# Places of a mixture of experts, due earlier and closer together in the order of an attention kernel

## The chip, the cores and the metric

The kernel runs on one core of one Trainium2 chip. The metric is the device time of one execution in microseconds (us). Before the change the median of 9 runs is 812.9 us (811.49 to 815.56).

## The reference

The input x has 2 batches of 2048 tokens of width 256, all in float32. First comes attention with 4 heads of width 64, with two layer norms ahead of it and a root-mean-square norm on queries and keys; its output is layer-normed and added to x. Then comes a mixture of 8 experts: each token goes through the one expert that its scores choose, and the result is layer-normed and added.

```python
x = x + _layernorm(_L0_attn_ref(_layernorm(x), ...))

scores = jnp.einsum('bsh,eh->bse', x, gate_w)
chosen = jnp.argmax(scores, axis=-1)
onehot = jax.nn.one_hot(chosen, gate_w.shape[0], dtype=x.dtype)
expert_out = jnp.einsum('bsh,efh->bsef', x, expert_w)
ffn = x + jnp.einsum('bsef,bse->bsf', expert_out, onehot)

x = x + _layernorm(ffn)        # ffn is fed with _layernorm(x)
```

## The kernel before, in words

Tokens stand in 32 tiles of 128. The attention is 256 steps (batch, block of 512 queries, pair of heads, tile of keys), taken two at a time: 128 loop passes, called slots here. In each slot the program emits, in this order: the scores of the next slot (`s`, L1049, on TensorE, or PE) with their exponentials (`p`, L1057, on ScalarE, or ACT); the addition of this slot's `p` into the running sum (`acc`, L1092 and L1094, on VectorE, or DVE); whatever side work is due (`between(now)`); and the product of `p` with the values (`po`, L1103, on PE). Instructions are emitted in a manual order, and each engine takes its own in that order and waits where an operand isn't there yet. So side work that is emitted ahead of a slot's `po` delays the `po` if it has to wait.

The side work is a set of Python generators. A queue holds each with the slot at which it begins. A `yield` ends its share of a slot; `yield later(...)` does too, while `then(...)` goes on in the same slot. In `places` the first part (the gather) is emitted as soon as the generator is taken up.

What the side work is:

- `project`: norm, queries, keys and values of a tile.
- `tokens`: a tile's output product (`py`, L802), norm, residual `x2`, expert scores, pick, and norm `x2n`. A tile of a group writes `x2` and `x2n` to memory.
- `order(gr)`: for a group of tiles, sorts the tokens by expert. Group A is tiles 0 to 15, group B tiles 16 to 27. It begins when the last tile of the group has its pick. Its first part (rank matmuls at L588 and L589, then some 24 small DVE operations) is one slot's work; its second part (L640 to L671, DVE, ending with the comparisons `inrow`) is the next slot's. Two `yield`s follow. Then PE turns it into the list of source rows (`src`, L681: 32 matmuls in group A, 24 in group B) and DVE casts it (L688). It then queues the places and the collects.
- `places(gr, j)`: one tile of 128 places that have one expert; A has 23, B has 19. GpSimd (POOL) gathers the rows (`rows`, L707), the SyncE queue (SP) loads the expert's weights (`ring`, L721), PE turns the rows (`pt_g`, L729), ACT copies them (`xT`, L734), PE multiplies (`pe`, L739; `peA`, `peB` by group), ACT copies out (L749), the norm follows (DVE L387 to L389; the root on POOL, L383 and L400, while attention runs, and on ACT, L404, or wholly on ACT, L414 to L424, after it), ACT scales (L755), and SP writes the result `fn` (L756).
- `collect(gr, t)`: gathers a tile's results from `fn` (L777, POOL), adds the residual (L789, DVE) and writes the output (L793). In group B it waits until all of `fn` is written.

The last four tiles, 28 to 31, are in no group: each goes through all 8 experts (L871, two products of four experts each) and DVE picks (L886, L888). After the last slot, `finish()` emits what is left in an order that it plans with a cost and a wait that each step states (`Next("POOL", 1.3)` and so on), and with counts of free buffers (`have`). So that order is a result of planned times, not of measured ones.

A place is due at slot `at`, which goes up by 1 for each place (by 0.34 past the attention's end).

Of the kernel before, what the change touches and what calls it, by code (L numbers as in the profile page):

```python
# [25 lines left out]
def kernel(  # L26
# [18 lines left out]
    B, N, D = x.shape  # L45
# [4 lines left out]
    NT = N // P  # L50
# [3 lines left out]
    QT4 = KB // P  # L54
# [227 lines left out]
    def bounded_path():  # L282
# [70 lines left out]
        def ps_m(name):  # L353
            return psum.tile([P, KB], F32, tag="ps_m", name=name, bufs=3)
# [20 lines left out]
        def later(*args, **kw):  # L375
            return Next(*args, later=True, **kw)
# [16 lines left out]
        def norm(src, name, shift=None, give=""):  # L393

            mv, rs = moments(src, name)
            if shift is None:
                shift = small.tile([P, 1], F32, tag="shift", name=f"shift_{name}")
            if attending:
                rsqrt(rs, mv[:, 1:2], 1.0, LN_EPS, ALU.add)
                nc.gpsimd.tensor_scalar(shift, mv[:, 0:1], rs, -1.0, ALU.mult, ALU.mult)  # L400
            else:
                yield then("ACT", 0.2, give=give)
                sd = small.tile([P, 1], F32, tag="sd", name=f"sd_{name}")
                nc.scalar.activation(sd, mv[:, 1:2], AF.Sqrt, bias=eps)  # L404
                yield then("DVE", 0.4)
                nc.vector.reciprocal(rs, sd)
                nc.vector.tensor_scalar(shift, mv[:, 0:1], rs, -1.0, ALU.mult, ALU.mult)
            return rs, shift

        def norm_on_act(dst, src, name):  # L410

            a = small.tile([P, 4], F32, tag="onact", name=f"onact_{name}")
            total, less, square, sd = (a[:, i : i + 1] for i in range(4))
            nc.scalar.activation(dst, src, AF.Copy, accum_out=total)  # L414
            nc.scalar.activation(less, total, AF.Copy, scale=-1.0 / D)
            sq = wk.tile([P, 2 * D], F32, tag="sq", name=f"sq_{name}", bufs=1)
            nc.scalar.activation(sq[:, :D], dst, AF.Square, bias=less, accum_out=square)
            nc.scalar.activation(sd, square, AF.Sqrt, bias=eps, scale=1.0 / D)
            yield then("DVE", 0.2, give="m")
            rs = small.tile([P, 1], F32, tag="rs", name=f"rs_{name}")  # L420
            nc.vector.reciprocal(rs, sd)
            yield then("ACT", 0.2)
            shift = small.tile([P, 1], F32, tag="shift", name=f"shift_{name}")
            nc.scalar.activation(shift, less, AF.Copy, scale=rs)  # L424
            return rs, shift
# [126 lines left out]
        def load_experts():  # L552
            nonlocal weD
            v = kv.tile([P, NT, DG], F32, tag="V", name="ring").rearrange("p t d -> p (t d)")
            ring.extend(
                v[:, i * KB : (i + 1) * KB].rearrange("p (c d) -> p c d", d=D)
                for i in range(NT // NCH)
            )
            xg = wk.tile([P, 6, D], F32, tag="rows", name="rows", bufs=1)
            rows.extend(xg[:, i, :] for i in range(6))  # L560
            weD = kv.tile([P, NCH, E, D], F32, tag="KT", name="weD")
            for e in range(E):
                nc.sync.dma_start(out=weD[:, :, e, :], in_=weTd[e])
            yield
# [17 lines left out]
        def order(gr):  # L582


            T, S, n = gr.T, gr.S, gr.name
# [89 lines left out]
                    ALU.is_equal,  # L675
                )
            yield
            yield
            ps = ps_m(f"src{n}")
            for t in range(T):  # L680
                nc.tensor.matmul(  # L681
# [5 lines left out]
                )  # L687
            nc.vector.tensor_copy(gr.src, ps[:, :S])  # L688

            at = now + 1  # L690
            for j in range(S):
                at += 0.34 if at >= len(steps) // PAIR + lead else 1
                g = opens(early(places(gr, j)), Next("POOL", 1.3), 0, lambda: 0.0 if ring and rows else None)
                queue.append((at, g))
            for t in range(T):
# [6 lines left out]
        def places(gr, j):  # L702

            n = f"{gr.name}{j}"
            assert ring and rows, "a tile of places with no room"
            w, xg = ring.pop(0), rows.pop(0)
            nc.gpsimd.indirect_dma_start(  # L707
                out=xg,
                out_offset=None,
                in_=gr.x2n[:, :],  # L710
                in_offset=bass.IndirectOffsetOnAxis(ap=gr.src[:, j : j + 1], axis=0),
                bounds_check=gr.T * P - 1,
                oob_is_err=False,
            )
            e = nc.values_load(
                gr.exp[0:1, j : j + 1],
                engines=[mybir.EngineType.SP],
                min_val=0,
                max_val=E - 1,
            )  # L720
            nc.sync.dma_start(  # L721
                out=w, in_=weTd[bass.ds(e, 1)].rearrange("e p c d -> p (e c) d")
            )
            yield later("PE", 0.3, 3.0, take="mx")
            if attending:
                yield later("PE", 0.3, take="mx", give="mx")
            pt = ps_m(f"pt_g{n}")
            for c in range(NCH):
                nc.tensor.transpose(  # L729
                    pt[:, c * P : (c + 1) * P], xg[:, c * P : (c + 1) * P], ident  # L730
                )
            yield then("ACT", 0.4)
            xT = wk.tile([P, NCH, P], F32, tag="xT", name=f"xT{n}", bufs=4)
            nc.scalar.copy(xT, pt[:, :D].rearrange("p (c n) -> p c n", n=P))  # L734
            rows.append(xg)
            yield later("PE", 0.9, take="mf", give="m")
            pe = ps_m(f"pe{n}")[:, :D]
            for c in range(NCH):
                nc.tensor.matmul(  # L739
                    pe, xT[:, c, :], w[:, c, :], start=(c == 0), stop=(c == NCH - 1)  # L740
                )
            ring.append(w)
            f = spare.pop() if spare else None
            own = f is None
            if own:
                f = wk.tile([P, D], F32, tag="fl", name=f"f{n}", bufs=5)
            yield then("ACT", 1.5 if j % 3 == 0 else 0.4, give="x")
            if attending or j % 3:
                nc.scalar.copy(f, pe)  # L749
                yield then("DVE", 0.7, give="m")  # L750
                scale, shift = yield from norm(f, f"f{n}")
            else:
                scale, shift = yield from norm_on_act(f, pe, f"f{n}")
            yield later("ACT", 0.6)
            nc.scalar.activation(f, f, AF.Identity, bias=shift, scale=scale)  # L755
            nc.sync.dma_start(out=gr.fn[j * P : (j + 1) * P, :], in_=f)  # L756
            gr.left -= 1
            gr.written = max(gr.written, clock + 2.5)
            yield later("", 0.0, 2.5)
            if not own:  # L760
                spare.append(f)
            yield later("", 0.0, give="f")
# [33 lines left out]
        def tokens(bt, qb, j, oTs, gr):  # L796
# [40 lines left out]
            if gr:  # L837
                gr.met += 1
                if gr.met == gr.T:
                    queue.append((now, order(gr)))  # L840
                    queue.sort(key=lambda q: q[0])
# [61 lines left out]
        def early(g):  # L903

            firsts.add(g)
            return g
# [84 lines left out]
        def opens(g, step, order, gate=None):  # L991


            opening[g], order_of[g] = step, order
            if gate:
                gates[g] = gate
            return g

        batches = [Batch(b) for b in range(B)]
        for t in range(NT):  # L1000
            queue.append((t, project(batches[0], t)))
        steps = [
            (b, qb, c, kc)
            for b in range(B)
            for qb in range(NKB)
            for c in range(NCH)
            for kc in range(NT)
        ]

        groups = []  # L1010
        for name, first, n in (("A", 0, NT), ("B", NT, NT - QT4)):
            groups.append(Group(name, n))
            groups[-1].first = first
        queue.append((NT + NT * NKB + 4, load_experts()))
        queue.append((0, weights()))
        queue.append((3, scale_g()))
# [2 lines left out]
        PAIR = 2  # L1019
# [94 lines left out]
        attending = True  # L1114
        now = lead = 0
# [4 lines left out]
        for g in range(len(steps) // PAIR):  # L1120
# [5 lines left out]
            lead = now - g  # L1126
# [9 lines left out]
            if kc == NT - 1:  # L1136
# [5 lines left out]
                if c == NCH - 1:  # L1142
                    tt = b * NT + qb * QT4
                    gr = next((g for g in groups if g.first <= tt < g.first + g.T), None)
# [9 lines left out]
        attending = False  # L1154
# [333 lines left out]
    with tc.If(chosen != 0) as cmp:  # L1488
        with ExitStack() as path:
            bounded_path()  # L1490
# [44 lines left out]
```

## Time and profile before

| what | value |
|---|---|
| median of 9 runs | 812.9 us |
| profiled execution, its time | 812.81 us |
| profiled execution, its span | 811.0 us |
| PE busy | 761.1 us, 94% |
| DVE busy | 640.0 us, 79% |
| ACT busy | 448.8 us, 55% |
| POOL busy | 326.7 us, 40% |
| last `po` of the attention ends | 722.65 us |

The profile is of one execution. Times in its timeline are from the span's start; a row gives the start, the duration, the engine, the line, the operation, output and input tiles with their shapes, and how many equal ones follow each other. A bracket at the end of a row is the idle time of the engine before it and what ended it. PEclk is the clock that TensorE was granted, as a share of full speed. The ends of matmuls are modelled.

### The profile page before, as it was taken

Reading aid. Unit: us, or ns where it says so; the run is one execution under the profiler, and the core shown is the slowest. Engines: PE = TensorE matmul, PEld = TensorE weight load, DVE = VectorE, ACT = ScalarE, POOL = GpSimd, SP = SyncE. Lnnn points to the kernel's source line nnn. Section 1 sums busy time; section 2 is a strip of 40 time slices with the busy share of each in tenths; the row PEclk is TensorE's granted clock in tenths of the full one; section 3 lists DMA queues with packets and bytes.
Section 4 is the critical chain, followed back from the end, with each engine's and each line's share of the span. In section 5 each row is a group of like instructions: output and inputs, shape, how many; then the busy total and the mean of one; then the engine's idle time right before and its main releaser. Section 6 shows DMA issues by size and latency. Waiting matters only on the chain.

```text
span 811.0 us, 10279 instructions
## 1 busy us (share of the span) xinstructions
PE 761.1 (94%) x3169; PEld 319.4 (39%) x3169; DVE 640.0 (79%) x1380; ACT 448.8 (55%) x699; POOL 326.7 (40%) x336
## 2 busy tenths in 40 slices
PE   6999999999999999999997999999999997985794
PEld 4555434433433433333332434444433232433451
DVE  3767678698879878788899958788789899953767
ACT  3666555556665665655554466656665534453741
POOL 4634411144353334242242236757454453244014
PEclk9999999999999999999999999999999998996897
DMA  4100111200100000000411423432222332436136
GB/s 127 54 27 26 52 66 52 65 27 20 46 20 20 20 14 20 20 21 24 126 33 46 131 66 117 120 114 87 58 66 85 117 98 81 135 119 185 53 98 185
DMA packets 48150, 57.58 MB, mean 71 GB/s; under 512 B 5868, under 2 KB 39416, under 8 KB 48088
## 3 DMA queue, kind: packets, MB, share of 16 engines
q1 hardware_dynamic: 41528, 44.65, 17.4%
q0 software_dynamic: 3568, 9.32, 4.7%
q10 hardware_dynamic: 2992, 2.88, 1.2%
q8 instruction: 27, 0.44, 0.2%
q14 instruction: 35, 0.29, 0.1%
HBM read 37.69 MB, written 19.14 MB: 70 GB/s over the span
## 4 chain that ended last, share of the span: by engine, by line
PE 76%; DVE 12%; issue 4%; ACT 3%; DMA 3%; POOL 1%; SPq 0%; DVEq 0%; POOLq 0%; ACTq 0%
PE s L1049 25%; PE po L1103 24%; PE pqk L463 7%; PE pv L472 4%; DVE acc L1094 3%; PE py L802 3%; PE peA L739 3%; PE pt_qk L500 2%; PE sm L1065 2%; PE peB L739 2%; PE pt_x L450 1%; DVE acc L1073 1%; PE pe L871 1%; DMA fgA<-fnA,posA 1%; DMA gk_all<-in_L_attn_k_gamma_dram 1%
## 5 line engine op out<-in xcount | busy, mean ns | idle before, releaser
L1057 ACT ACTIVATE p<-s,nbound 128x1024 f32<-128x1024 f32 x256 | 271.0, 1110 | 182.8 <-PE s L1049 182.8
L1094 DVE TENSOR_TENSOR acc<-acc,p 128x1024 f32<-128x1024 f32 x224 | 273.7, 1222 | 11.5 <-ACT p L1057 1.2
L1049 PE MATMUL s<-QT,KT 64*128 64x512 f32 x1024 | 255.7, 618 | 2.3 <-ACT p L1057 2.3
L1103 PE MATMUL po<-p,V 128*64 128x512 f32 x1024 | 251.5, 612 | 0.2 <-ACT oT L1138 0.2
L1049 PEld LDWEIGHTS s<-QT,KT 64*128 64x128 f32 x1024 | 88.5, 187 | 166.2 <-issue 92.2
L1103 PEld LDWEIGHTS po<-p,V 128*64 128x64 f32 x1024 | 64.0, 137 | 128.8 <-issue 126.4
L383 POOL TENSOR_TENSOR rn<-rs_t,mhalf 128x8 f32<-128x8 f32 x32 | 58.8, 1838 | 72.7 <-DVE rs_t L382 72.7
L383 POOL TENSOR_TENSOR roots<-rs_t,mhalf 128x1 f32<-128x1 f32 x32 | 23.9, 747 | 93.3 <-DVE rs_t L382 93.1
L463 PE MATMUL pqk<-wqkT,xnT 128*128 128x512 f32 x128 | 60.8, 598 | 0.6 <-ACT xnT L454 0.6
L383 POOL TENSOR_TENSOR rs_z<-rs_t,mhalf 128x1 f32<-128x1 f32 x28 | 34.8, 1244 | 59.0 <-DVE rs_t L382 59.0
L383 POOL TENSOR_TENSOR rs_y<-rs_t,mhalf 128x1 f32<-128x1 f32 x28 | 32.1, 1148 | 55.7 <-DVE rs_t L382 49.2
L1073 DVE RECIPROCAL acc<-acc 128x128 f32<-128x128 f32 x45 | 42.5, 945 | 0.0
L846 ACT ACTIVATE x2n<-x,shift_y,rs_y 128x256 f32<-128x256 f32 x28 | 16.8, 599 | 44.3 <-POOL shift_y L400 39.5
L802 PE MATMUL py<-woT,oT 128*128 128x264 f32 x128 | 36.9, 413 | 3.8 <-issue 3.3
L707 POOL DMA_INDIRECT rows<-x2nA,srcA x23 | 29.8, 1297 | 24.3 <-DVE srcA L688 18.3
L777 POOL DMA_INDIRECT fgA<-fnA,posA x16 | 19.9, 1242 | 37.7 <-DVE rs_t L382 12.0
L472 PE MATMUL pv<-wvT,xnT 128*128 128x264 f32 x128 | 33.7, 386 | 0.0
L1073 DVE RECIPROCAL acc<-sm 128x128 f32<-128x128 f32 x19 | 18.1, 951 | 18.8 <-PE sm L1065 17.3
L383 POOL TENSOR_TENSOR rs_fA<-rs_t,mhalf 128x1 f32<-128x1 f32 x23 | 18.0, 785 | 36.0 <-DVE rs_t L382 35.0
L472 PEld LDWEIGHTS pv<-wvT,xnT 128*128 128x128 f32 x128 | 24.3, 190 | 17.4 <-issue 11.0
L777 POOL DMA_INDIRECT fgB<-fnB,posB x12 | 12.4, 1038 | 46.5 <-DMA fgB<-x2B 43.1
L802 PEld LDWEIGHTS py<-woT,oT 128*128 128x128 f32 x128 | 22.5, 194 | 19.9 <-issue 16.4
(265 smaller groups left out, 932.1 us busy)
## 6 DMA issues: line engine op xcount, KB each, us to landing
ring<-weTd SPq DMA_DIRECT2D x34, 256.0 KB
x<-in_L_attn_x_dram SPq DMA_DIRECT2D x8, 512.0 KB
xr<-in_L_attn_x_dram SPq DMA_DIRECT2D x28, 128.0 KB
fnA<-fA SPq DMA_DIRECT2D x23, 128.0 KB
we_raw<-in_L_ffn_expert_w_dram ACTq DMA_DIRECT2D x8, 256.0 KB
weTd<-weT SPq DMA_DIRECT2D x8, 256.0 KB
x2A<-x SPq DMA_DIRECT2D x16, 128.0 KB
fgA<-x2A SPq DMA_DIRECT2D x16, 128.0 KB
```

The lines of the kernel that those rows point to most:

```text
L383: nc.gpsimd.tensor_tensor(dst, t[:, :n], mhalf[:, :n], ALU.pow)
L463: nc.tensor.matmul(pqk, xnT[:, c, :], wqkT[:, c, :, :].rearrange("p a d -> p (a d)"), start=(c == 0), stop=(c == NCH - 1),)
L472: nc.tensor.matmul(pv[:, :DG], xnT[:, c, :], wvT[:, c, :], start=(c == 0), stop=(c == NCH - 1),)
L707: nc.gpsimd.indirect_dma_start(out=xg, out_offset=None, in_=gr.x2n[:, :], in_offset=bass.IndirectOffsetOnAxis(ap=gr.src[:, j : j + 1], axi ...
L739: nc.tensor.matmul(pe, xT[:, c, :], w[:, c, :], start=(c == 0), stop=(c == NCH - 1))
L777: nc.gpsimd.indirect_dma_start(out=o, out_offset=None, in_=gr.fn[:, :], in_offset=bass.IndirectOffsetOnAxis(ap=gr.pos[:, t : t + 1], axis= ...
L802: nc.tensor.matmul(py, oT[:, bass.ts(j, P)], woT[:, c, :], start=(c == 0), stop=(c == NCH - 1),)
L1049: nc.tensor.matmul(s[:, r, :], bt.KT[rows, c, bass.ts(kc, P)], bt.QT[qb][rows, c, :], start=True, stop=True,)
L1057: nc.scalar.activation(p, s, AF.Exp, bias=nbound)
L1073: nc.vector.reciprocal(acc[:, 0, cols], share[:, cols])
L1094: nc.vector.tensor_tensor(acc, acc, p, ALU.add)
L1103: nc.tensor.matmul(po[r * DH : (r + 1) * DH, :], batches[b].V[:, kc, h * DH : (h + 1) * DH], p[:, r, :], start=(kc == 0), stop=(kc == NT - 1),
```

## The change

Four places of the program change:

- `order` has one `yield` less between its second part and `src`. This holds for both groups.
- A group has a `pace`: 1 for A, 0.6 for B. The first place is due at `now + 1` in place of `now + 2`, and in B each later one 0.6 of a slot after the one before, so five in three slots.
- In B, the extra step of one slot between the gather and the turn of its rows, while attention runs, is left out.
- `collect` is queued after the places as before, so its due slots move with them.

```diff
                     ALU.is_equal,
                 )
             yield
-            yield
             ps = ps_m(f"src{n}")
...
-            at = now + 1
+            at = now + 1 - gr.pace
             for j in range(S):
-                at += 0.34 if at >= len(steps) // PAIR + lead else 1
+                at += 0.34 if at >= len(steps) // PAIR + lead else gr.pace
...
             yield later("PE", 0.3, 3.0, take="mx")
-            if attending:
+            if attending and gr.pace == 1:
                 yield later("PE", 0.3, take="mx", give="mx")
...
-        for name, first, n in (("A", 0, NT), ("B", NT, NT - QT4)):
+        for name, first, n, pace in (("A", 0, NT, 1), ("B", NT, NT - QT4, 0.6)):
             groups.append(Group(name, n))
-            groups[-1].first = first
+            groups[-1].first, groups[-1].pace = first, pace
```

## The prediction

> **What bounds the kernel now.** I read the chain of waits first, then PE's timeline around the three places that the change touches, then DVE's beside it, and last the windows with PE's clock.
>
> ```profile
> PE 76%; DVE 12%; issue 4%; ACT 3%; DMA 3%; POOL 1%; SPq 0%; DVEq 0%; POOLq 0%; ACTq 0%
> ```
>
> PE is three quarters of the chain. Up to 722.65, where the last `po` ends, it hardly rests: between 440 and 606 it is busy for 165.27 of 166 us. There, a wait of PE adds to the end in full, and so does work added to PE. After 722.65 comes a tail of 88.4 us (811.05 - 722.65), in which PE waits on ACT, gathers and clock. The change moves work from the tail into the full part and moves two matmul groups (`src`) closer to what they wait for.
>
> **Part 1: `srcA` one slot earlier.** The timeline of PE, then of DVE:
>
> ```profile
> 440.84 1.99 PE L1049 MATMUL s<-QT,KT 64*128 64x512 f32 x8
> 443.56 1.08 PE L1065 MATMUL sm<-acc,ones 128*64 128x512 f32 x4 [0.73 <-DVE acc L1094]
> 444.47 1.89 PE L1103 MATMUL po<-p,V 128*64 128x512 f32 x8
> 446.28 1.99 PE L1049 MATMUL s<-QT,KT 64*128 64x512 f32 x8
> 448.20 3.75 PE L681 MATMUL srcA<-idsA,inrowA 128*128 128x23 f32 x32
> 451.88 1.94 PE L1103 MATMUL po<-p,V 128*64 128x512 f32 x8
> ```
> ```profile
> 446.71 2.49 DVE L671 TENSOR_TENSOR inrowA<-rowA,col 128x512 f32<-128x512 f32 x4
> ```
>
> The built program's order puts `srcA` now between the `s` of 440.84 and `sm`. That `s` ends at 442.76; the first of the four `inrowA` is done at 446.71 + 0.68 = 447.4, and nothing ahead of it on DVE moves. So PE waits 4.65 us, runs `srcA` (3.68 us) to 451.1, and then has `sm`, `po`, `s` (0.91 + 1.81 + 1.92) still to do: the `po` of 451.88 starts at 455.7. That is 3.85 us lost, with the old wait of 0.73 us already in it. Queued behind the waiting matmuls are `sm` and every later `po`; DVE waits behind it too, with its cast of `srcA`, but it has only 3.75 us of work in such a slot of 3.79 and isn't late.
>
> Then the clock. The windows, with PE's busy time and the granted clock behind it:
>
> ```profile
> 430.05:433.46 3.41, 0.53 (x4) 1.00 0.21 57
> 433.46:436.87 3.41, 3.41 (x10) 0.50 0.17 58
> 692.87:696.29 3.42, 3.42 (x28) 1.00 0.75 210
> 696.29:699.70 3.41, 3.41 (x10) 0.50 0.76 204
> ```
>
> A stretch of 3.41 us with 0.53 busy is followed by one at half speed. So is the stretch of 692.87, which looks full: 2.55 us of it are `srcB`'s small matmuls. So a wait of 4.65 us with 3.7 us of small matmuls behind it should cost two or three such stretches. A 128x128 turn starts 136 ns after the one before at full clock and 214 ns at half (744.77); `srcA`'s matmuls start 0.115 us apart, so I take 0.21 at half, which adds up to 3.1 us; and what remains of the last half-speed stretch behind it adds 0.6 to 1.5. If `srcA` were not slowed at all, only 1.4 behind it would remain. Clock: 0 to 4.7 us (nothing, if the stretches fall luckily), taken at 3.85, nearest to the row after the 4.18 us wait for `rankA`, where everything ran at half. **Part 1: +7.7 (3.85 to 8.6).** No gain: A's places were hidden among slots before and are now.
>
> The Trainium skill ("TensorE: Matmul & The Clock Gate", "HAM oscillation") warns of PE idle gaps over some 3.4 us. By that rule A's gap pays and B's below, of 2.8 us, doesn't (0.8 us off the sum); the row of 692.87, with no gap in it, says that small matmuls pay too, and I go by the row.
>
> **Part 2: group B up to the last `po`.** The collects of A come two slots earlier. So the gather on POOL (664.68) that delays the root of tile 27's norm is gone, and with it DVE's idle 0.45 us before its `x2`: `rankB` comes 0.45 earlier. Two additions of A (L789 at 680.29 and 687.85, 0.40 each) leave DVE between there and `inrowB`, which is done 1.25 earlier in all.
>
> ```profile
> 687.99 1.08 PE L1065 MATMUL sm<-acc,ones 128*64 128x512 f32 x4
> 692.63 2.85 PE L681 MATMUL srcB<-idsB,inrowB 128*128 128x19 f32 x24
> 695.42 2.86 PE L1103 MATMUL po<-p,V 128*64 128x512 f32 x8
> ```
>
> `srcB` now stands ahead of that `sm`. PE comes to it at 687.97 - 0.45 = 687.5; the first `inrowB` (691.57 before) is there at 690.3. Wait: +2.8. The gather of place 0 starts with the cast at about 693 in place of 698, its turn at about 701 in place of 712.2: eight us are enough for a landing, as 698.02 to 712 was.
>
> In the built order nine turns and seven products of B stand ahead of the last `po`, before it was three and two. So five products (0.97 each, as 716.35 to 717.32) and six turns (0.31) come into the full part: +6.7. ACT has room: a slot with two places costs it 2.12 for `p` and some 2.4 for copies and scaling, in 6.2 us. The wait and `srcB` make a poor stretch of 5.6 us, which costs 1.7 to 3.6 in half clock, by where in it the stretches of 3.41 begin, 2.4 on average, where `srcB` costs 1.64 now (`po` 2.79 for 1.87, `s` 2.64 for 1.92): +0.8 (-1.6 to +2.4). **Part 2: -0.45 + 2.8 + 6.7 + 0.8 = +9.85.**
>
> **Part 3: the tail.**
>
> ```profile
> 722.65 1.13 PE L739 MATMUL peB<-ring,xTB 128*128 128x256 f32 x4
> 742.90 2.07 PE L739 MATMUL peB<-ring,xTB 128*128 128x256 f32 x4 [3.27 <-issue]
> 744.77 1.46 PE L729 MATMUL pt_gB<-ident,rows 128*128 128x128 f32 x4
> 778.36 20.81 PE L871 MATMUL pe<-weD,kept 128*128 128x512 f32 x48
> ```
> ```profile
> 721.42 0.60 ACT L755 ACTIVATE fB<-fB,shift_fB,rs_fB 128x256 f32<-128x256 f32 x1 [3.15 <-POOL shift_fB L400]
> ```
>
> From 722.65 to 744.77 stand just five products, places 2 to 6: a poor stretch, with waits for gathers and two of 3.3 us that no row explains. All five are now ahead of the tail: -22.1. In their place is a new start: the scaling of places 4 to 6 stands on ACT ahead of the copies for places 7 and on, and waits for POOL's roots (1.47 + 0.86 at 718.95, 0.56 + 0.26 at 723.23, one after the other, with gathers of 1.3 between), as in the ACT row above: some 2.3 and then 2.7 us, +5 (2.3 to 11, where the two unexplained waits come again).
>
> From 744.77 to 778.36 the same twelve places, 7 to 18, follow in both orders, in 33.6 us. Two expert products of tile 28 stand among them before (5.1 + 3.4 us) and none now, while `sm` and three `py` (4.0 us) come in. If PE set the pace, that would be -4.6, or up to -8.6 where those four fall into waits; if ACT sets it (10.8 and 11.7 busy in each 15 us), nothing. I take -4. After 778.36 six expert products run back to back, and the end comes 32.7 us later. There are now eight: +2 x 3.44, less some 1.1, since the collects, whose additions stand at the very end (806.39), are through by then: +5.8. **Part 3: -22.1 + 5 - 4 + 5.8 = -15.3.**
>
> **Sum:** 7.7 + 9.85 - 15.3 = +2.25 on the profiled execution's 812.81 (span 811.0, and 1.8 around it): 815.06. That execution stands 0.1 under the median of 812.9, so I forecast **815.0 us**.
>
> **Rivals.**
>
> - *The tail gives more (faster).* One mechanism: between places 7 and 18 PE's order, not ACT, sets the pace, so that the two expert products taken out give back all of 8.6, and the new start costs only its first wait, 2.3. The tail is -22.1 + 2.3 - 8.6 + 5.8 = -22.6, the sum -5: 807.8, and 805 with Part 1 at its clock's lower half. For it: ACT was idle for 1.9 us at `pt_f`, waiting for PE. Against: ACT's busy share there. It decides from a tail gain of 19.2 on. Chance 0.28.
> - *No clock is lost.* `srcA` and `srcB` run at full speed in their new places: 3.85 less, and 0.8 less in B. 810.4, up to 812 with one stretch lost. For: a single stretch more or less is chance. Against: the rows above. Chance 0.15, taken as no change.
> - *The tail keeps its poor start (slower still).* The two unexplained waits come again behind the last `po`, since eight gathers and the weights still go out at once: start +11 in place of +5, 821. Chance 0.17.
> - *Nothing moves* is excluded: the order of the built program shows the places ahead of the last `po`.
>
> **How the numbers follow.** Forecast 0.40 (its own range 814.5 to 818), rivals 0.28, 0.15, 0.17. A measurement tells about 0.2% from no change, 811.3 to 814.5 here. Slower 0.40 + 0.17 = 0.57, same 0.15, faster 0.28. The range reaches into the first and the last rival until about one in ten is left out at each end: 806.5 to 822.
>
> **What would show it.** Part 1: a row of `srcA` with an idle time of some 4.6 us on `inrowA` before it, and a window at half clock there; without it the step is wrong. Part 2: some 2.8 us before `srcB`, and the last `po` of the attention at 722.65 + 7.7 + 9.85 = 740.2. Part 3: from that `po` to the span's end 73 us in place of 88.4, ACT waiting for POOL's `shift_fB` at its start, and the expert products in one block of some 28 us. A last `po` before 735 or a tail under 69 would make the forecast wrong on the fast side, a tail over 78 on the slow.

## The result

The changed kernel takes 820.23 us (median of 20 runs, 817.55 to 825.55), the kernel before on the same chip 813.13 us (62 runs). The ratio is 1.0104, 95% interval 1.0086 to 1.0122: slower by 7 to 10 us. The forecast of 815.0 had the sign and lay 5.2 us too low; the range of 806.5 to 822 holds the time. The profiled execution took 822.17 us (span 820.4) and so lies 1.9 us above its median, which has to be kept in mind where traces are subtracted.

The shares of the chain of waits in the profile after:

```profile
PE 73%; DVE 14%; issue 3%; ACT 3%; DMA 3%; POOL 3%; SPq 0%; POOLq 0%; DVEq 0%; ACTq 0%
```

PE has lost 3 points, DVE and POOL have gained 2 each. Ahead of both `src` the chain now runs through DVE's work up to `inrow`. PE's timeline around both `src` shows it (start, duration, engine, line, operation, tiles, count, and the idle time before in brackets):

```profile
442.12 1.99 PE L1048 MATMUL s<-QT,KT 64*128 64x512 f32 x8
448.04 6.43 PE L680 MATMUL srcA<-idsA,inrowA 128*128 128x23 f32 x32 [3.93 <-DVE inrowA L671]
454.40 1.98 PE L1064 MATMUL sm<-acc,ones 128*64 128x512 f32 x4
456.16 3.27 PE L1102 MATMUL po<-p,V 128*64 128x512 f32 x8
...
687.63 0.74 PE L588 MATMUL rankB<-picksB,before 128*128 128x96 f32 x2 [5.14 <-DVE picksB L279]
...
701.19 5.24 PE L680 MATMUL srcB<-idsB,inrowB 128*128 128x19 f32 x24 [3.69 <-DVE inrowB L671]
706.36 1.98 PE L1064 MATMUL sm<-acc,ones 128*64 128x512 f32 x4
708.12 3.59 PE L1102 MATMUL po<-p,V 128*64 128x512 f32 x8
...
745.11 1.94 PE L1102 MATMUL po<-p,V 128*64 128x512 f32 x8
```

Both `src` wait for `inrow`, and both, with the `sm` and `po` behind them, take 1.7 to 1.9 times as long as before (`srcA` 3.75, `srcB` 2.85, `sm` 1.08, `po` 1.89). The windows of PE there tell why. In every trace here the granted clock changes only at steps of 3.41 us; one such step is called a stretch. The rows have (stretch, its length, PE's busy time and instructions, granted clock, DMA share, GB/s):

```profile
445.30:448.71 3.41, 0.68 (x6) 1.00 0.49 97
448.71:452.12 3.41, 3.41 (x18) 0.50 0.76 251
452.12:455.54 3.42, 3.42 (x15) 0.50 0.74 219
455.54:458.95 3.41, 3.41 (x10) 0.50 0.39 118
697.88:701.29 3.41, 0.10 (x1) 1.00 0.22 37
701.29:704.71 3.42, 3.42 (x17) 0.50 0.70 204
704.71:708.12 3.41, 3.41 (x14) 0.50 0.73 227
708.12:711.53 3.41, 3.41 (x10) 0.50 0.71 239
```

In this execution three stretches at half clock follow each wait. The first stands behind the wait. It is filled with `src`'s small matmuls and is followed by a second, which still holds 1.6 to 2.3 us of them, and that one by a third. Three is not the rule: in two runs below (group A of e3, group B of e2) only two follow waits of 3.44 and 3.33 us, by where the stretches fall.

I set the start of every slot's `po` beside that of before. The difference is 0.6 us from the first slot on, 1.3 behind `rankA`, 9.4 behind `srcA`, 10.4 ahead of `rankB`, 9.5 behind it, 16.9 behind `srcB` and 24.3 at the end of the last `po` (746.97 in place of 722.65). From there to the span's end it is 73.4 us in place of 88.4. The scaling at the start of that tail on ACT, and the experts at its end on PE:

```profile
743.69 0.60 ACT L754 ACTIVATE fB<-fB,shift_fB,rs_fB 128x256 f32<-128x256 f32 x1 [2.36 <-POOL shift_fB L400]
745.59 0.60 ACT L754 ACTIVATE fB<-fB,shift_fB,rs_fB 128x256 f32<-128x256 f32 x1 [1.30 <-POOL shift_fB L400]
749.45 0.60 ACT L754 ACTIVATE fB<-fB,shift_fB,rs_fB 128x256 f32<-128x256 f32 x1 [1.78 <-POOL shift_fB L400]
```
```profile
780.05 5.26 PE L870 MATMUL pe<-weD,kept 128*128 128x512 f32 x8 [0.46 <-ACT kept L859]
...
804.41 7.11 PE L870 MATMUL pe<-weD,kept 128*128 128x512 f32 x16 [0.56 <-DVE kept L887]
```

### The profile page after: what moved, and what is told of

It is laid out like the page before. It is cut to its first block, busy times and chain, and to the rows that moved or that the text cites. A ratio compares the mean times of both kernels' runs of the same rounds, so it can differ in the third digit from the quotient of the medians.

```text
span 820.4 us, 10298 instructions
## 1 busy us (share of the span) xinstructions
PE 769.6 (94%) x3169; PEld 325.1 (40%) x3169; DVE 641.0 (78%) x1381; ACT 446.2 (54%) x684; POOL 338.1 (41%) x346
## 4 chain that ended last, share of the span: by engine, by line
PE 73%; DVE 14%; issue 3%; ACT 3%; DMA 3%; POOL 3%; SPq 0%; POOLq 0%; DVEq 0%; ACTq 0%
PE po L1102 23%; PE s L1048 23%; PE pqk L463 7%; DVE acc L1093 4%; PE pv L472 3%; PE peA L738 3%; PE pe L870 3%; PE py L801 3%; PE pt_qk L500 2%; PE sm L1064 2%; PE peB L738 1%; PE pt_x L450 1%; DVE acc L1072 1%; DMA x<-in_L_attn_x_dram 1%; ACT p L1056 1%
## 5 line engine op out<-in xcount | busy, mean ns | idle before, releaser
L383 POOL TENSOR_TENSOR rs_z<-rs_t,mhalf 128x1 f32<-128x1 f32 x28 | 36.7, 1310 | 62.5 <-DVE rs_t L382 62.4
L870 PE MATMUL pe<-weD,kept 128*128 128x512 f32 x64 | 30.1, 623 | 1.5 <-ACT kept L859 0.9
L472 PEld LDWEIGHTS pv<-wvT,xnT 128*128 128x128 f32 x128 | 24.3, 190 | 17.4 <-issue 11.0
L387 DVE BATCH_NORM_STATS2 st_fA<-fA 128x6 f32<-128x256 f32 x23 | 9.8, 426 | 27.3 <-ACT fA L748 27.3
```

The lines of the kernel that those rows point to most:

```text
L383: nc.gpsimd.tensor_tensor(dst, t[:, :n], mhalf[:, :n], ALU.pow)
L472: nc.tensor.matmul(pv[:, :DG], xnT[:, c, :], wvT[:, c, :], start=(c == 0), stop=(c == NCH - 1),)
L870: nc.tensor.matmul(pes[:, r].rearrange("p e d -> p (e d)"), xT[:, c, :], weD[:, c, e + r * EB : e + (r + 1) * EB, :].rearrange("p e d -> p ...
```

## The experiments

My theory after the result: the `yield` taken from `order` costs what the pace of the places brings, and more, by the wait at `src` and by the clock behind it. The rivals: the places themselves cost it, or the wait alone does and the clock is chance. The first four runs had a common kernel before of 813.39 us, the next four one of 813.5, the last two one of 813.47.

**e1: both groups get the second slot back** (the changed kernel with its `yield` returned; the pace stays):

```diff
             yield
+            yield
             ps = ps_m(f"src{n}")
```

> The changed kernel with the second yield ahead of src put back, in both groups; the pace of 0.6 and the missing gather step stay. Theory (the loss is PE's wait for inrow ahead of src and the half clock that follows it, 8.1 us in group A and 7.4 us in group B): some 15.5 us less than the changed kernel, less about 1 to 3 for one place fewer ahead of the last po, so 805 to 808, faster than before. Rival (the loss is the places moved into the full part, 7.5 us of PE, and ACT's waits for POOL): hardly better than the changed kernel, 816 to 819.

Measured: 807.66 us, ratio 0.9914 (0.9893 to 0.9935). Faster than both kernels, by 7.0 us than before. Neither `src` waits, `srcA` takes 3.75 and `srcB` 2.85 us. The places cost nothing on balance; the `yield` does.

**e2: only group A gets it back:**

```diff
             yield
+            if gr.pace == 1:
+                yield
             ps = ps_m(f"src{n}")
```

> The changed kernel with the second yield put back in group A alone. A's places hang on nothing later, so only the wait ahead of srcA goes. Theory: 8.1 us less than the changed kernel, 811 to 813. Rival (places moved): no difference, 819 to 821.

Measured: 813.59 us, 0.9991 (0.9974 to 1.0008). So the `yield` costs 9.2 us in A (1.0104 - 0.9991) and 6.3 in B (0.9991 - 0.9914, of 813), by the intervals each within some 2 us. In B of this trace PE waits 3.33 us, two stretches at half follow, and the slots lose 5.4 us there.

**e3: the kernel before with one `yield` less, nothing else:**

```diff
             yield
-            yield
             ps = ps_m(f"src{n}")
```

> The kernel before with one yield less ahead of src, in both groups, and nothing else of the change. Three products of group B stand ahead of the last po in place of two. Theory: 8.1 and 7.4 us more, less some 3 for the place moved, so 824 to 827, slower than the whole change. Rival: the yield by itself is harmless, 811 to 814.

Measured: 826.1 us, 1.013 (1.0096 to 1.0165), so +10.6 us. In its trace the slots come 6.0 us later behind `srcA` (a wait of 3.44 us and two stretches at half) and 7.3 behind `srcB` (3.93 us and three). The cost is there without any new pace.

**e4: the wait filled with turns of 128x128** (28 in A, 22 in B; what they write is overwritten by `src`):

```diff
             ps = ps_m(f"src{n}")
+            for _ in range(28 if gr.pace == 1 else 22):
+                nc.tensor.transpose(ps[:, :P], ident, ident)
             for t in range(T):
```

> The changed kernel with 28 (group A) and 22 (group B) turns of the identity emitted ahead of the src matmuls, into the same PSUM tile, which src then overwrites: they fill PE's wait and take no operand from DVE. The wait for inrow stays, the idle time doesn't. If half of the loss is the clock (src takes 6.4 and 5.2 us in place of 3.7 and 2.8, and what follows is at half speed), some 4.3 us in A and 4 to 5 in B come back: 811 to 813. If the clock isn't held by such turns, or small matmuls count as idle anyway, 818 to 821.

Measured: 817.74 us, 1.0044 (1.0025 to 1.0063), between what the two theories had, nearer to the second. The windows of PE in group A of this kernel tell where the theory was too simple:

```profile
443.16:446.57 3.41, 3.07 (x28) 1.00 0.02 5
446.57:449.99 3.42, 2.17 (x20) 1.00 0.75 192
449.99:453.40 3.41, 3.41 (x17) 0.51 0.83 232
453.40:456.81 3.41, 3.41 (x10) 0.50 0.80 243
```

The first stretch holds the turns, and the clock behind it is full. The second holds the rest of the wait (1.25 us) and `srcA`'s matmuls; that one is followed by half clock. So turns of 128 columns hold the clock, and 2.2 us of `src`'s matmuls of 23 columns beside that rest don't, though both follow each other by about 0.12 us. The rows without a wait, below, tell the matmuls from the wait.

**e9: the wait filled with four matmuls of 128x512** (a product of the identity with weights, overwritten likewise):

```diff
             ps = ps_m(f"src{n}")
+            for _ in range(4):
+                nc.tensor.matmul(ps, ident, wqk2[:, 0, :], start=True, stop=True)
             for t in range(T):
```

> The changed kernel with four matmuls of 128x512 (a product of the identity with weights, overwritten by what follows) ahead of the source products of either group, where PE waits for inrow: they fill the wait with wide matmuls as the attention has them. Theory that the clock falls by what the array does in the wait: it stays full, the source products take 3.7 and 2.8 us instead of 6.4 and 5.2, the offsets at the first and second source fall from 8.1 and 7.4 to about 4 each: 811 to 813.5 us. Rival that the narrow source products themselves drop the clock: the half-clock stretch stands behind them all the same, 815 to 818 us. Rival that the clock has nothing to do with the wait: 819 to 821 us.

Measured: 817.33 us, 1.0044 (1.0015 to 1.0074). The same as with the turns, so 128 or 512 columns make no difference that shows. Groups A and B go different ways. PE's rows, A first:

```profile
444.71 3.70 PE L680 MATMUL srcA<-wqkT,ident 128*128 128x512 f32 x8
449.43 4.56 PE L682 MATMUL srcA<-idsA,inrowA 128*128 128x23 f32 x32 [1.01 <-DVE inrowA L671]
...
697.17 3.70 PE L680 MATMUL srcB<-wqkT,ident 128*128 128x512 f32 x8
700.71 2.79 PE L682 MATMUL srcB<-idsB,inrowB 128*128 128x19 f32 x24
703.42 1.08 PE L1066 MATMUL sm<-acc,ones 128*64 128x512 f32 x4
```

And PE's windows:

```profile
448.76:452.17 3.41, 2.74 (x25) 1.00 0.79 227
452.17:455.58 3.41, 3.41 (x14) 0.50 0.83 232
...
701.40:704.80 3.40, 3.40 (x27) 1.00 0.77 201
704.80:708.20 3.40, 3.40 (x18) 1.00 0.79 233
```

In B the wait of 3.69 us is replaced by 3.70 us of work that nobody needs, so the time waited is the same, and only the clock differs: `srcB`, `sm` and `po` run at full speed, and the slots lose 2.2 us there (9.2 to 11.4) where the changed kernel loses 7.4. **The difference of 5.2 us between these two executions is the clock alone.** In A a whole stretch is `srcA` with a rest of the wait (0.67 us), and the clock falls behind it all the same. So each theory of this run has its result in one group.

A contrast from e1, with no wait at all: `srcB`'s 2.85 us fell into one stretch there, and it paid.

```profile
695.80:699.20 3.40, 3.40 (x28) 0.99 0.74 193
699.20:702.60 3.40, 3.40 (x10) 0.51 0.82 221
```

In the run above the same 2.79 us lay across the boundary of two stretches, 0.7 and 2.1 us, and were free. These stretches lie on a fixed grid of 3.41 us within a run, whose phase differs from run to run. All the `src` that PE met without a wait agree: there are 15, in before, e1, e2 (A), e5, e6, e8, e10 and e11. In seven, one stretch held 2.39 to 3.36 us of them, and the next was at half; in eight, none held more than 2.33, and the next was at full clock. So the narrow matmuls themselves drop the clock where a stretch holds enough of them, the second theory of this run, and B was spared by the phase.

**e8: the step between gather and turn returned** (e1 with the old condition, so that the pace alone is new):

```diff
-            if attending and gr.pace == 1:
+            if attending:
                 yield later("PE", 0.3, take="mx", give="mx")
```

> Two slots from the picks to the places as in e1, and the extra step between a gather and its turn kept; only the pace of the places is new. By the theory that the step less from a gather to its turn costs PE nothing and moves one place ahead: 808 to 811 us, the last po some 2 us earlier than in e1 and the tail some 3 to 4 us longer. Rival: the turn that comes one step earlier waits for its gather, and without it the kernel is faster: 804 to 807 us.

Measured: 809.69 us, 0.9949 (0.9924 to 0.9975). The pace alone brings 4.1 us (2.0 to 6.2 by the interval). The step less brings some 2.8 more by the two ratios, but the two intervals meet (0.9924 and 0.9935), so I don't call it shown.

**e6: a faster pace on e1:**

```diff
-(("A", 0, NT, 1), ("B", NT, NT - QT4, 0.6))
+(("A", 0, NT, 1), ("B", NT, NT - QT4, 0.4))
```

> Two slots from the picks to the places as in e1, and the second group's expert products at two in five slots' pace of 0.4 a product instead of 0.6, so that more of them lie ahead of the last attention slot. If the tail still pays for each product moved: the tail loses some 3 us per product moved and the part ahead gains some 2.5: 804 to 807 us. Rival: the tail is by now bound by the experts' own products, one block of which stands behind the other, and each product moved ahead costs there what it saves here: 807 to 810 us.

Measured: 814.59 us, 1.0017 (0.9991 to 1.0043), worse than either had said. PE's row in its tail, and ACT's:

```profile
774.85 1.33 PE L855 MATMUL pt_f<-ident,kept 128*128 128x128 f32 x4 [10.71 <-issue]
```
```profile
767.48 1.08 ACT L755 ACTIVATE fB<-fB,shift_fB,rs_fB 128x256 f32<-128x256 f32 x2
768.46 0.84 ACT L404 ACTIVATE sd_z<-mv_z,eps 128x1 f32<-128x1 f32 x4
...
774.20 1.24 ACT L846 ACTIVATE kept<-x,shift_y,rs_y 128x256 f32<-128x256 f32 x2
```

PE stands still for 10.71 us. The last four tiles' norms (`sd_z`) come on ACT behind the scaling of the last places, and their scores, picks and `kept` follow until 774.2; the profile says "issue", but `pt_f` reads `kept`, so I take the wait to be for that. With every place through, PE has nothing left to do beside that chain. So the pace pays only as long as places remain to cover it.

**e5: the rank products one slot later, too** (on e1):

```diff
         def order(gr):
+            yield
             T, S, n = gr.T, gr.S, gr.name
```

> Two slots from the picks to the places as in e1, and the rank product one slot later too, in both groups. If PE's waits ahead of the rank products (4.2 us in the first group with a half-clock stretch behind it, 5.2 us in the second with another) are losses of the same kind as those ahead of srcA and srcB, they go: some -6 and -7, less 2 to 3 for the second group's places one slot later: 797 to 803 us, offset of the slots against the kernel before near -5 after the first group's places and -10 after the second's. Rival: the wait comes back at the sources, since the picks come late by themselves and the slot in between is too short: 807 to 812 us.

Measured: 817.24 us, 1.0043 (1.0016 to 1.007). My theory fell, and the rival's place was wrong too. The wait at `rankA` did go, and the slot there came 4.7 us earlier. But PE's rows and ACT's behind it:

```profile
433.61 0.49 PE L589 MATMUL rankA<-picksA,before 128*128 128x128 f32 x2
...
453.00 3.79 PE L1050 MATMUL s<-QT,KT 64*128 64x512 f32 x8 [6.55 <-ACT p L1058]
```
```profile
451.45 0.48 ACT L1078 COPY acc<-sm 128x384 f32<-128x384 f32 x1 [10.20 <-DVE acc L1074]
```

The places' arithmetic on DVE now stands ahead of the reciprocals of a finished head (L1074). ACT waits for them for 10.2 us, with the exponentials queued behind, and PE for those. The wait came back elsewhere, with the half clock behind it.

**e10 and e11: wide matmuls ahead of the rank products**, where PE waits 4.2 and 5.2 us in both kernels; e10 is e1 with them, e11 the kernel before with them (what they write is overwritten):

```diff
             ps = ps_m(f"rank{n}")
+            for _ in range(4 if n == "A" else 5):
+                nc.tensor.matmul(ps, ident, wqk2[:, 0, :], start=True, stop=True)
```

> The kernel with two slots from picks to places (e1), with four (first group) and five (second group) matmuls of 128x512 ahead of the rank products, where PE waited 4.2 and 5.2 us for the picks; what they write is overwritten. Theory that 3.4 us without wide matmuls give half the clock in the stretch behind: the half-clock stretches of 6.8 us behind either rank product go or shrink, the slots behind come some 2 to 3 us earlier in each group, 802 to 805 us. Rival that the fill delays the rank products or that the clock falls all the same: 807 to 810 us.

> The kernel before with the same four and five wide matmuls ahead of its rank products and nothing else. Theory of the clock: its half-clock stretches behind the rank products (3.4 us in the first group, 6.8 us in the second) go, 1.7 and 3.4 us of loss with them: 808 to 811 us. Rival: no change or a loss by the fill, 813 to 815 us.

Measured: 806.25 us on e1, 0.9927 (0.99 to 0.9954), which can't be told from e1's 0.9914; and 812.67 us on the kernel before, 1.0006 (0.9975 to 1.0036), no change. And yet the mechanism worked. In e1 with the filling:

```profile
433.20 0.46 PE L590 MATMUL rankA<-picksA,before 128*128 128x128 f32 x2 [0.54 <-DVE picksA L279]
433.49 0.39 PE L591 MATMUL rankA<-picksA,allones 128*128 128x128 f32 x2
433.81 1.94 PE L1105 MATMUL po<-p,V 128*64 128x512 f32 x8
...
443.82 1.08 PE L1067 MATMUL sm<-acc,ones 128*64 128x512 f32 x4 [2.37 <-DVE acc L1096]
```

The `po` behind `rankA` takes 1.94 us where it took 3.68 in e1, and PE is 3 us ahead one slot later. Then it waits 2.37 us for DVE, and a stretch at half follows that wait. The windows from `rankA` and `rankB` to those `sm`, and the one behind the first (PE, PEld, DVE, ACT, POOL):

```profile
433.80:443.80 10.00, 7.65 (x33) 2.35 (x32) 9.28 (x29) 5.42 (x6) 2.35 (x2) 1.00 0.10 32
443.80:450.10 6.30, 6.28 (x20) 1.74 (x20) 6.09 (x14) 0.00 (x0) 0.00 (x0) 0.73 0.42 125
679.70:689.80 10.10, 7.64 (x35) 2.35 (x34) 9.37 (x31) 5.42 (x6) 2.35 (x2) 1.00 0.08 26
```

DVE is busy for 9.28 of 10 us and PE for 7.65. Between the picks and `src`, DVE sets the pace, and a faster PE only waits longer for it. Group A of e11 shows it with no stretch at half anywhere near, so that a clock lost again behind the new wait isn't the reason there:

```profile
445.10 1.08 PE L1067 MATMUL sm<-acc,ones 128*64 128x512 f32 x4 [2.37 <-DVE acc L1096]
```

Its slots are 1.7 us ahead behind `rankA`, this wait is 2.37 us where it was 0.73, and the next `po` is back where it was (1.54 us behind that of before, 1.58 at the start). That also tells why the half clock behind the rank products cost nothing by itself: DVE takes that time anyway.

## Why the prediction was right in sign and too low

**Part 1, `srcA`: right.** Predicted +7.7; the slots show 9.40 - 1.28 = +8.1, the run with A's slot returned +9.2. Of the 8.1, the wait is 3.2 (3.93 less the old 0.73; predicted 3.85) and the clock 4.9 (predicted 3.85). The mechanism is the predicted one; that the sum is so near is partly luck, since the two errors nearly cancel, and e3 has 6.0 for the same step.

**Part 2, `srcB`: the failing step, a term that was sized too small.** It reads "a poor stretch of 5.6 us, which costs 1.7 to 3.6 in half clock ... where `srcB` costs 1.64 now: +0.8". The trace shows 16.86 - 9.46 = +7.4 from wait and clock together, where the prediction had 2.8 + 0.8 = 3.6. The wait is 3.7 in place of 2.8. It grew because PE came to it 0.9 us earlier than predicted: only one stretch at half stood behind `rankB` and not two, and DVE didn't come earlier with it. The clock's net share is then 7.4 - 3.7 = 3.7 in place of 0.8, or 5.3 with the 1.64 of before. My stretch was measured as if `srcB` ran at full speed. But the first half-clock stretch lengthens `srcB` from 2.79 to 5.24 us, so the next stretch is poor as well, and a third at half follows. The wide filling in B, which takes the clock's part away and leaves the time waited, puts this term at 5.2 us. It differs between executions: by wait and slots e3 has 5.0 in B and e2, with two stretches, 3.7 (5.4 - 3.33 + 1.64). Both are above the 2.4 that was put there on average.

**The 0.45 us at `rankB`: not seen.** The wait there is 5.14 us after 5.17. The reading that the gather in the way would be gone was wrong: one of A's gathers still stands on POOL ahead of a root there (675.08), and DVE still idles 0.44 us for that root (679.38).

**Places in the full part: nearly right.** Predicted +6.7; 24.32 - 16.86 = +7.5. It includes a wait for a gather, which the prediction put at nothing:

```profile
744.76 0.41 PE L728 MATMUL pt_gB<-ident,rows 128*128 128x128 f32 x2 [1.23 <-DMA rows<-x2nB,srcB]
```

**Tail: right.** Predicted -15.3, measured 73.4 - 88.4 = -15.0. The waits at its start for `shift_fB` sum to 5.4 us (2.36 + 1.30 + 1.78) where 5 was taken. The twelve places with that start took 33.1 us (746.97 to 780.05) where 34.6 was implied, and from the experts' block to the end it is 40.3 us where 38.5 was: the block itself takes 31.5 us (780.05 to 811.52) where some 28 was given, its first product 5.26 us at half clock.

**Not foreseen:** 0.6 us at the start, 0.7 of clock behind `rankA`, 1.0 more between the groups. The first two differ from trace to trace (the start lies 0.0 us, e5, to 2.0 us, e9, behind that of before). The 1.0 is one wait of PE that before doesn't have, ahead of a `po` whose `oT` stood on ACT behind an `x2n` that waited 3.33 us for POOL's `shift_y`:

```profile
618.80 1.94 PE L1102 MATMUL po<-p,V 128*64 128x512 f32 x8 [0.97 <-ACT oT L1137]
```

So +24.3 ahead of the last `po` in place of +17.55, and -15.0 behind it. Most of the miss of 6.8 is the 3.8 at `srcB`. Of the rivals, none came true: the clock was lost, the tail gave neither more nor less. The range reached up to 822 because of the rival with a poor start of the tail (821). That the measured time lies next to that rival's figure is luck: the miss came at `srcB`, and the tail was as forecast. Its list of signs had a gap: a last `po` before 735 was to count against it, but no bound stood on the late side, and the miss came there.

On the rule: the Trainium skill ("TensorE: Matmul & The Clock Gate", "HAM oscillation") speaks of idle gaps over some 3.4 us. Both gaps here, 3.93 and 3.69 us, are over that, and both paid, so they agree with it. Two rows don't follow from it: `srcB` in e1, with no gap, and `srcA` behind the wide filling, with 0.7 us idle in its stretch, paid too.

## What to carry to other kernels

Before a dependent product is moved closer to its operands, compare the path of the engine that makes them with the room that is left: here DVE's chain from picks to `inrow` sets the earliest time, and a slot taken away comes back as PE's wait, with 3 to 5 us of half clock behind a wait of under 4. Take the good half of such a change alone: the closer places with the slot kept are 7 us faster than before (0.9914). Before filling a wait or speeding up one engine, see who is busy in that window; where another has 9.3 of 10 us, nothing is won.

## What the hardware showed that was not expected

- Enough small matmuls in a stretch drop the clock though the profile shows PE fully busy: one with 2.39 us of 128x19 matmuls (695.80 in e1) was followed by one at half, one with 2.33 us of 128x23 (447.11 in before) wasn't; turns of 128x128 (443.16 in e4, busy for 3.07 us) kept it full.
- It depends on how they fall on the grid of 3.41 us: of 2.79 us, 2.39 in one stretch cost a stretch at half (e1), and 2.1 in one, the rest across a boundary, nothing (e9, group B).
- At half clock a 128x23 matmul starts about 0.2 us after the one before (6.43 us for 32) in place of 0.115, so the poor stretch lengthens itself.
